# Replacing one of sixteen gathers per block by one-hot products on TensorE, in both layers of a graph network

## The chip, the cores and the metric

The kernel runs on one core of one Trainium2 chip. The metric is the device time of one execution, in microseconds (us), as the median of several. The engines of the core are called PE (TensorE), DVE (VectorE), ACT (ScalarE), POOL (GpSimd, which here issues the indirect DMAs) and SP (SyncE, which here issues nearly all other DMAs).

## The reference

A two-layer graph network with residuals: 6250 nodes of 128 features, 200000 edges `src -> dst`, sorted by `dst`. Everything is float32.

```python
h = jnp.maximum(_layernorm(x, axis=-1), 0.0)
x = x + _L0_gnn_ref(h, src, dst, W, attn_l, attn_r, bias)     # attention, 8 heads of 16
h = jnp.maximum(_layernorm(x, axis=-1), 0.0)
x = x + _L1_gnn_ref(h, edge_attr_4, edge_attr_8, ...)         # tensor product messages

# _L0_gnn_ref
z = (feat @ W).reshape(N, HEADS, PER_HEAD)
el = jnp.einsum('nhp,hp->nh', z, attn_l)
er = jnp.einsum('nhp,hp->nh', z, attn_r)
e = jax.nn.leaky_relu(el[src] + er[dst], negative_slope=NEG_SLOPE)
emax = jax.ops.segment_max(e, dst, num_segments=N)
a = jnp.exp(e - emax[dst])
denom = jax.ops.segment_sum(a, dst, num_segments=N)
agg = jax.ops.segment_sum(z[src] * a[:, :, None], dst, num_segments=N)
out = agg / jnp.maximum(denom, 1e-09)[:, :, None] + bias

# _L1_gnn_ref: s, v = up-projected node features; h = two silu layers on 8 edge features; tpw = h @ A3
mji = concat([ss*y_s*w0, dot(vs, y_v)/R3*w3, ss*y_v*w1, vs*y_s*w2])   # per edge, 256 numbers
message = jax.ops.segment_sum(mji, receiver, num_segments=num_nodes) / 10.0
# then two output projections
```

What matters here is that both layers need, for every edge, the row of a node table at the edge's source: `z[src]` with `el[src]` (136 numbers) in layer 0, `s, v` at `src` (128 numbers) in layer 1. The sources are random.

## The kernel before

**Tiling.** The edges are cut into 1563 tiles of 128 (one edge per partition) and these into 98 blocks of 16 tiles (`KB`). Since edges are sorted by destination, a block's destinations lie in a window of 128 nodes, and two blocks complete one tile of 128 nodes. Segment sums are products with one-hot matrices: `one_hot` (L1097) compares the block's local destination numbers with a row of 0 to 127, and `sums` (L1234, layer 0) or `sums1` (L1570, layer 1) multiplies that with the weighted rows, summing a block in a PSUM bank.

**Rows of the sources.** The node table of layer 0, `t0`, is computed at the start and written to DRAM, 544 bytes a row; that of layer 1, `t1`, is written tile after tile while layer 0 ends its nodes. `gather` (L833) is one indirect DMA on POOL per tile: 128 rows to 128 partitions. `take_rows` issues a block's gathers three steps ahead in layer 0 and two in layer 1, into the five buffers of `z_pool`; block 0 has a buffer of its own, and layer 1's first 24 tiles use another, early table with late corrections. In every third block (`by_row`: 3, 6 up to 93) tile 15 is not gathered: SP fetches its 128 rows by 128 plain DMAs whose addresses come from registers, loaded 32 at a time (`rows_by_row`, L1078). `rows_until` paces this at 42.67 rows per block, so that it is done some eight blocks before the layer's end, and `filled` (ACT) copies the rows to their place.

**Order of the work.** In both loops PE, DVE, ACT and SP execute in the order in which the program writes the instructions; POOL has its own order, of gathers. A step g of layer 0's loop works on four blocks at once:

- block g: `logits` (L1176 to L1179, needs the gathered rows and `er` at the destination), `maxima`;
- block g−1: `neighbours`, `weights`, `weighted` (L1229), `sums`, and, in every second step, the end of a node tile (`node_x` to `node_s`, `node_out` writing `t1` and `t1z`, L1298);
- block g+1: `masks_of`, `turned` (L1151, L1153: the sixteen one-hots of the block are transposed on PE, four to a bank, and cast by ACT), `er_of` (products of the turned one-hots with `er3`);
- block g+2: `ends_of`, the one-hots on DVE.

On SP a step issues: rows, the last node tile's writes, the load of a tile of `x` (L1239, into `x_all`, which stays in SBUF), rows. Layer 1 goes by units of four tiles: `network` for the next block (L1516, L1520), `tensor_weights` (L1533, L1537), `messages` (L1553 to L1562), `sums1` (L1570), and `node1`.

**Before the loops**, tables and masks are prepared: `a1p` (L1001) and the destinations `d_c` (L1025), `d_i` are loaded, local destinations and masks formed (L1141 picks a block's masks by a product).

Of the kernel before, what the change touches and what calls it, by code (L numbers as in the profile page):

```python
# [741 lines left out]
def tile_even_edges(  # L742
# [88 lines left out]
    def gather(to, table, tiles, width, first=0):  # L831
        for k, t in enumerate(tiles, first):
            nc.gpsimd.indirect_dma_start(  # L833
                out=to[:, k, :width], out_offset=None, in_=table,
                in_offset=bass.IndirectOffsetOnAxis(ap=src_col[:, t : t + 1], axis=0))
        return to
# [128 lines left out]
def even_edges(tc, v):  # L965
# [7 lines left out]
    with ExitStack() as ctx:  # L973
        const = ctx.enter_context(tc.tile_pool(name="fconst", bufs=1))
        z_pool = ctx.enter_context(tc.tile_pool(name="fz", bufs=5))
        s_pool = ctx.enter_context(tc.tile_pool(name="fs", bufs=16))
        row_pool = ctx.enter_context(tc.tile_pool(name="frow", bufs=3))
        of_l0 = ctx.enter_context(ExitStack())
        l0c = of_l0.enter_context(tc.tile_pool(name="l0c", bufs=1))

# [14 lines left out]
        x_all = const.tile([P, NX, P], F32, name="fx_all")  # L995
# [8 lines left out]
        a3p = const.tile([P, 2, P], F32, name="fa3p")  # L1004
        nc.sync.dma_start(a3p, v["a3p"])
# [4 lines left out]
        wout = const.tile([P, 2, P], F32, name="fwout")  # L1010
        nc.sync.dma_start(wout, v["wout"])
        dloc = const.tile([P, NB * KB], F32, name="fdloc")
        identb = l0c.tile([P, P], BF, name="fidentb")
        nc.vector.tensor_copy(identb, ident)
# [8 lines left out]
        with tc.tile_pool(name="fbuild", bufs=1) as build:  # L1023
# [10 lines left out]
            nc.vector.tensor_sub(dloc[:, :TU], d_c, off)  # L1034

# [20 lines left out]
        with tc.tile_pool(name="fat_ps", bufs=1, space=PSUM) as at_ps:  # L1056
            col = l0c.tile([P, P], F32, name="fcol")
# [36 lines left out]
        def one_hot(t, m, iota=iota):  # L1094

            s = s_pool.tile([P, 4, P], F32, name="s")
# [20 lines left out]

        in_order = {mybir.EngineType.PE, mybir.EngineType.DVE, mybir.EngineType.Activation,
                    mybir.EngineType.SP}
        with tc.manual_schedule(engines=in_order), \  # L1120
                tc.tile_pool(name="l0", bufs=2) as l0, \
                tc.tile_pool(name="l0n", bufs=2) as l0n, \
                tc.tile_pool(name="l0_ps", bufs=1, space=PSUM) as l0_ps:
# [3 lines left out]
            p_n = l0_ps.tile([P, 512], F32, name="p_n")  # L1127
            er_p, iota_p = p_n[:, P : 2 * P].rearrange("p (t h) -> p t h", h=H), p_n[:, 3 * P :]
            nc.scalar.copy(iota_p, iota)

# [14 lines left out]

            def turned(c, q):
                if 4 * q < c["kt"]:
                    m = min(4, c["kt"] - 4 * q)
                    p_d = l0_ps.tile([P, 4, P], F32, name="p_d", bufs=2)
                    for k in range(m):  # L1150
                        nc.tensor.transpose(p_d[:, k, :], c["s"][q][:, k, :], ident)  # L1151
                    d = c["d", q] = l0.tile([P, 4, P], BF, name="d", bufs=4)
                    nc.scalar.copy(d[:, :m], p_d[:, :m])  # L1153
# [17 lines left out]
            def logits(c, bank="pe"):  # L1171
# [3 lines left out]
                pe = c["pe"] = p_n if bank == "p_n" else l0_ps.tile([P, 512], F32, name=bank, bufs=2)  # L1175
# [61 lines left out]

            def node_rows(i, n):
                nc.sync.dma_start(x_all[:, i : i + n, :],  # L1239
                                  xp[i * P : (i + n) * P].rearrange("(j p) f -> p j f", p=P))  # L1240

            def with_bias(i, n):
                x_i = x_all[:, i : i + n, :]
                nc.vector.tensor_add(x_i, x_i, bias_b[:, None, :].to_broadcast([P, n, F]))

            def node_x(u):
                i, n, agg = u["i"], u["n"], u["agg"]
                x_i = x_all[:, i : i + n, :]
# [14 lines left out]
            def node_h(u):  # L1263
                i, n = u["i"], u["n"]
                rs, mr = normal(l0n, u["mv"], u["rs"], n, f"n{n}")
                xn = u["xn"] = l0n.tile([P, 2, P], F32, name="xn")
                nc.scalar.activation(xn[:, 0, :], x_all[:, i, :], AF.Identity, bias=mr[:, 0, :],
                                     scale=rs[:, 0, :])
                if n == 2:
                    nc.vector.tensor_scalar(xn[:, 1, :], x_all[:, i + 1, :], u["mv"][:, 1, 0:1],  # L1270
                                            rs[:, 1, :], op0=OP.subtract, op1=OP.mult)

            def node_t(u):
                n = u["n"]
                u["p_n"] = p_n.rearrange("p (j f) -> p j f", f=P)
                for j in range(n):
                    nc.tensor.transpose(u["p_n"][:, j, :], u["xn"][:, j, :], ident)
                h_t = u["h_t"] = l0n.tile([P, 2, P], F32, name="h_t")
                nc.scalar.activation(h_t[:, :n], u["p_n"][:, :n], AF.Relu)
# [11 lines left out]
            def node_out(u):  # L1291
                i, n, sv = u["i"], u["n"], u["sv"]
                first = i * P - W0
                for table in (t1, t1z) if i < LATE else (t1,):
                    if i == 0:
                        nc.sync.dma_start(table[: P - W0, :], sv[W0:, 0, :])
                    else:
                        nc.sync.dma_start(  # L1298
                            table[first : first + n * P].rearrange("(j p) f -> p j f", p=P), sv)

# [12 lines left out]
            def take_rows(g):  # L1313
                if 0 < g < NG:
                    c = cs[g]
                    t = c["b"] * KB + c["o"]
                    c["z"] = gathered(t0, range(t, t + c["kt"] - (c["b"] in by_row)), ZW)
# [28 lines left out]
            for g in range(1, 3):  # L1346
                take_rows(g)
            masks_of(cs[0])
# [12 lines left out]
            for i in range(2):  # L1361
                node_rows(i, 1)
            for g in range(NG - 3):
# [3 lines left out]
                for n in late:  # L1367
                    node_out(n)
                if g % 2 == 0 and g // 2 + 2 < NX - 2:
# [6 lines left out]
                logits(c)  # L1376
                ends_of(n2, 0)
# [3 lines left out]
                maxima(c)  # L1381
                ends_of(n2, 1)
# [5 lines left out]
                er_of(n1, 0)  # L1388
                if b4:
                    weights(b4)  # L1390
                for n in nodes:
# [3 lines left out]
                if b4:  # L1395
                    bank_of(b4)
                    weighted(b4, 0)
                turned(n1, 3)
                er_of(n1, 2)
                if b4:  # L1400
                    weighted(b4, 8)
                for n in nodes:
# [4 lines left out]
                if b4:  # L1407
                    sums(b4, 0)
                for n in nodes:
# [7 lines left out]
                if b4:  # L1417
                    sums(b4, 8)
                if g == NG - 4:
# [68 lines left out]
        with tc.manual_schedule(engines=in_order), \  # L1488
                tc.tile_pool(name="l1", bufs=3) as l1, \
                tc.tile_pool(name="l1n", bufs=2) as l1n, \  # L1490
                tc.tile_pool(name="l1_ps", bufs=2, space=PSUM) as l1_ps:

# [8 lines left out]
            def network(b, step):  # L1501
# [7 lines left out]
                if step == 3 or 2 * q0 + 8 >= KT[b] and second:  # L1509
                    c["yp"] = held[:, P + b % 3 * KB * 3 : P + (b % 3 + 1) * KB * 3].rearrange(  # L1510
# [61 lines left out]

            def node1(i, agg):
# [274 lines left out]
```

## Time and profile before

| | |
|---|---|
| time, median of 3 | 3887.06 us (3886.89 to 3891.37) |
| the profiled execution: its own time | 3888.67 us |
| its span, first to last instruction | 3886.9 us |
| mean granted PE clock, share of full | 0.803 |
| gathers and their line | 3024 at L833 in groups of g, 2856.7 us |
| PE, DVE, ACT, POOL busy | 2848.8, 2224.5, 1396.8, 2913.0 us |
| rows by register on SP | 3968 a layer, 0.5 KB each |

How to read it. The busy line gives the time in which each engine executed, its share of the span, and its number of instructions (x). PEld is the loading of weights on PE, beside the matmuls. In the row of slices the span is cut in 40 parts, and a digit is the busy share in tenths; PEclk is the granted clock of PE in tenths. In a row of a group, `L833 POOL DMA_INDIRECT g<-ft,fsrc x3024 | 2856.7, 945 | 922.4 <-issue 858.3` reads: line, engine, operation, output and inputs by the program's names, count, then busy us and mean ns of one, then the idle time of the engine just before these instructions and what ended most of it; "issue" is time in which the engine waited for nothing that the profile shows. Tile numbers are left out of names: `ft` stands for the tables t0 and t1, `r` for the rows by register. A row of waits gives engine, tile, line and who released it, then us in total, times, and the longest. SP's issuing is no busy time on the page; its queue (SPq) is seen in the timeline, whose rows give start and length in us.

### The profile page before, as it was taken

How to read it: one execution, taken by the hardware profiler on the slowest of the kernel's cores; microseconds unless marked ns; L12 is line 12 of the kernel's file. 1: busy time of each engine (PE TensorE's matmuls, PEld its weight loads, DVE VectorE, ACT ScalarE, POOL GpSimd, SP SyncE). 2: the span in 40 equal slices, each digit the busy share in tenths (PEclk: the TensorE clock that was granted, in tenths of full speed). 3: DMA queues.
4: the chain of work that ended last, by engine and by line, in shares of the span. 5: the costliest groups of instructions: out<-in, count | busy, mean ns of one | idle time of the engine just before them, and what ended most of it. 6: DMA issues, size and time to landing. Idle time of an engine off the chain costs nothing. (4 is left out here: it accounts for less than half of the span.)

```text
span 3886.9 us, 62701 instructions
## 1 busy us (share of the span) xinstructions
PE 2848.8 (73%) x14785; PEld 2401.2 (62%) x14785; DVE 2224.5 (57%) x5408; ACT 1396.8 (36%) x3612; POOL 2913.0 (75%) x3096
## 2 busy tenths in 40 slices
PE   3766666666666766666678888888877777778777
PEld 3656656656556656666666666666666556656665
DVE  5544444444444444444457777677766666666666
ACT  3323232323322323232324444444444444444443
POOL 6777777777777777777777777777777777777776
PEclk6666666666666566666689999999999999999999
DMA  6222222222222222222222222222222222222221
GB/s 181 59 64 64 62 64 64 64 62 64 62 64 62 64 61 64 62 64 62 61 61 61 61 62 62 62 62 62 62 62 62 62 62 61 63 60 63 61 61 50
DMA packets 195262, 252.65 MB, mean 65 GB/s; under 512 B 78656, under 2 KB 145088, under 8 KB 194880
## 3 DMA queue, kind: packets, MB, share of 16 engines
q0 software_dynamic: 98048, 207.27, 22.6%
q1 hardware_dynamic: 96544, 41.19, 4.1%
q8 instruction: 120, 1.97, 0.2%
q14 instruction: 262, 2.15, 0.2%
q10 hardware_dynamic: 288, 0.07, 0.0%
HBM read 234.73 MB, written 13.25 MB: 64 GB/s over the span
## 5 line engine op out<-in xcount | busy, mean ns | idle before, releaser
L833 POOL DMA_INDIRECT g<-ft,fsrc x3024 | 2856.7, 945 | 922.4 <-issue 858.3
L1570 PE MATMUL p_u<-mj,s 128*128 128x256 f32 x3126 | 789.9, 397 | 217.9 <-DVE mj L1562 216.5
L1570 PEld LDWEIGHTS p_u<-mj,s 128*128 128x128 f32 x3126 | 588.9, 196 | 385.7 <-DVE mj L1562 310.9
L1234 PE MATMUL p_u<-g,s 128*128 128x136 f32 x3062 | 597.8, 376 | 0.4 <-DVE g L1229 0.4
L1234 PEld LDWEIGHTS p_u<-g,s 128*128 128x128 f32 x3062 | 572.1, 279 | 0.5 <-DVE g L1229 0.4
L1537 ACT ACTIVATE p_w<-p_w,yb 128x64 f32<-128x64 f32 x1563 | 450.3, 288 | 121.5 <-PE p_w L1533 80.4
L1553 DVE TENSOR_TENSOR vy<-g,p_i 128x384 f32<-128x384 f32 x387 | 212.9, 550 | 366.6 <-DMA g<-ft,fsrc 258.0
L1533 PE MATMUL p_w<-fa3p,h 128*128 128x256 f32 x1564 | 412.0, 387 | 0.0
L1151 PE MATMUL p_d<-fident,s 128*128 128x128 f32 x1563 | 384.7, 411 | 0.0
L1533 PEld LDWEIGHTS p_w<-fa3p,h 128*128 128x128 f32 x1564 | 289.4, 195 | 118.1 <-issue 52.5
L1176 DVE TENSOR_TENSOR e_s<-g,p_n 128x128 f32<-128x128 f32 x96 | 27.5, 286 | 578.6 <-DMA g<-ft,fsrc 566.2
L1518 ACT ACTIVATE h<-p_h,fb 128x512 f32<-128x512 f32 x196 | 134.6, 687 | 573.2 <-PE p_h L1516 571.8
L1151 PEld LDWEIGHTS p_d<-fident,s 128*128 128x128 f32 x1563 | 312.4, 225 | 37.6 <-issue 26.3
L1144 ACT COPY mk<-p_m 128x385 f32<-128x385 f32 (+1 forms) x99 | 47.6, 481 | 781.3 <-PE p_m L1141 781.2
L1229 DVE TENSOR_TENSOR g<-g,pe 128x1024 f32<-128x1024 f32 x193 | 225.5, 1209 | 129.2 <-ACT g L1220 126.4
L1153 ACT CAST d<-p_d 128x512 bf16<-128x512 f32 x391 | 228.8, 586 | 192.0 <-PE p_d L1151 141.6
L1179 PE MATMUL pe<-fident,e_s 128*128 128x128 f32 x98 | 39.1, 399 | 326.2 <-DVE e_s L1177 326.2
L1097 DVE TENSOR_TENSOR s<-p_n,fdloc 128x512 f32<-128x512 f32 x391 | 266.1, 682 | 6.7 <-ACT sv L1289 3.4
L1097 DVE TENSOR_TENSOR s<-p_i,fdloc 128x512 f32<-128x512 f32 x391 | 266.1, 681 | 3.8 <-ACT p_i L1512 3.8
L1516 PE MATMUL p_h<-ft,fa1p 128*128 128x128 f32 x1568 | 217.2, 283 | 63.3 <-DMA ft<-in_e_f_dram 63.1
L1516 PEld LDWEIGHTS p_h<-ft,fa1p 128*128 128x128 f32 x1568 | 210.6, 198 | 83.9 <-issue 65.3
L1523 ACT ACTIVATE h<-p_h,fb 128x512 f32<-128x512 f32 x196 | 134.7, 687 | 307.1 <-PE p_h L1520 307.1
(202 smaller groups left out, 3344.3 us busy)
## 6 DMA issues: line engine op xcount, KB each, us to landing
r<-ft SPq DMA_DIRECT2D x3968, 0.5 KB
r<-ft SPq DMA_DIRECT2D x3968, 0.5 KB
g<-ft,fsrc POOLq DMA_INDIRECT x3024
ft<-in_e_f_dram SPq DMA_DIRECT2D x98, 64.0 KB
yb<-in_e_y_dram SPq DMA_DIRECT2D x98, 32.0 KB
fx_all<-in_e_xp_dram SPq DMA_DIRECT2D x48, 64.0 KB
out_dram<-fx_all SPq DMA_DIRECT2D x47, 64.0 KB
ft<-sv SPq DMA_DIRECT2D x46, 64.0 KB
```

The source lines that it names most:

```text
L833: nc.gpsimd.indirect_dma_start(out=to[:, k, :width], out_offset=None, in_=table, in_offset=bass.IndirectOffsetOnAxis(ap=src_col[:, t : t + ...
L1097: nc.vector.tensor_tensor(s[:, :m], iota[:, None, :].to_broadcast([P, m, P]), dloc[:, t : t + m].unsqueeze(2).to_broadcast([P, m, P]), OP. ...
L1151: nc.tensor.transpose(p_d[:, k, :], c["s"][q][:, k, :], ident)
L1153: nc.scalar.copy(d[:, :m], p_d[:, :m])
L1229: nc.vector.tensor_mul(zh, zh, p_a[:, k0 : k0 + m].unsqueeze(3).to_broadcast([P, m, H, D]))
L1234: nc.tensor.matmul(c["p_u"][:, :ZW], c["s"][k // 4][:, k % 4, :], c["z"][:, k, :], start=c["o"] + k == 0, stop=c["o"] + k == KT[c["b"]] - 1)
L1516: nc.tensor.matmul(p_h[:, q, :], a1p[:, q0 + q, :], c["ft"], start=True, stop=True)
L1523: nc.scalar.activation(h2, p_h, AF.Silu, bias=b2)
L1533: nc.tensor.matmul(w[:, k : k + n].rearrange("p k a u -> p (k a u)"), c["h2"][q // 4][:, q % 4, :], a3p[:, :n].rearrange("p k f -> p (k f) ...
L1537: nc.scalar.activation(w[:, k, ::2, :], w[:, k, ::2, :], AF.Copy, scale=c["yb"][:, k0 + k, 0:1])
L1553: nc.vector.tensor_mul(vy, v_n, y_p)
L1570: nc.tensor.matmul(blk[b]["p_u"][:, :MW], u["s"][:, k, :], u["mj"][:, k, :], start=k0 + k == 0, stop=k0 + k == KT[b] - 1)
```

## The change

**Products in place of a gather.** In 44 blocks of layer 0 (`dense`: from block 27 on, those not in `by_row`) and in 20 of layer 1 (`dense1`: 16, 20, up to 92), tile 14 (`KD`) is no longer gathered. Its 128 rows are made by products. `spread` lays the tile's source numbers along the free axis by a product; `ends_to` compares them with the node numbers of 17 ranges and gives 17 one-hot matrices in bf16; `rows_of` multiplies each with the table, which lies in SBUF in three bf16 parts whose sum is the float32 number: 17 x 3 matmuls, each with up to three node tiles as columns (48 with 408 columns and 3 with 272 in layer 0; 384 and 256 in layer 1), summed in bank `p_x`. `taken` picks the right one of the three node tiles by three masks on DVE and writes the rows in place. In layer 0 this is spread over two steps, in layer 1 over five units (`dense_step`).

**The tables in three parts.** `node_tiles` loads two node tiles on SP, `in_three` splits them by two copies on ACT and two subtractions on DVE: a pair per step in the first 25 steps of layer 0, a pair per two units in the first 50 units of layer 1, with the load issued a step or four units ahead.

**The turned ends.** In layer 0 `turned` no longer transposes and casts. Four comparisons on DVE (128x512) compare a broadcast of the block's destinations with the partition's number. The broadcast is a load on SP per block, `ends_row`: a row of 4096 bytes of a new DRAM table `fends_d` to all 128 partitions, two buffers, issued after `logits` two blocks ahead. The table is written at the start, from a subtraction on DVE.

**Other moves.** `x` is no longer held in SBUF for both layers: layer 0 loads a tile per node tile and writes the sum to a DRAM table `fx1`, from which layer 1 loads it. Constant rows and columns that products need are held in a PSUM bank of their own. Some pools and constants move to the layer that uses them.

```diff
     def gather(to, table, tiles, width, first=0):
-        for k, t in enumerate(tiles, first):
+        for t in tiles:
+            k = first + t - tiles[0]
...
+            d_b = build.tile([P, TG, P], BF, name="fd_b")
...
+            nc.vector.tensor_sub(d_b, d_i, off_t.unsqueeze(2).to_broadcast([P, TG, P]))
+            nc.sync.dma_start(ends.rearrange("g t e -> t g e"), d_b)
...
+        NR = -(-NX // 3)
+        KD = KB - 2
+        order = sorted(range(NR), key=lambda k: (k > 0, 2 * NR + k < NX, k))
+        half = (NR + 1) // 2
+        dense = {b for b in range(NX // 2 + 2, NB - 4) if b not in by_row}
+        dense1 = set(range(NX // 4 + 4, NB - 4, 4))
...
+        def node_tiles(pool, table, width, i, n, bufs=2):
+            zr = pool.tile([P, 2, width], F32, name="zr", bufs=bufs)[:, :n]
...
+                nc.sync.dma_start(zr, rest.rearrange("(j p) f -> p j f", p=P))
+            return zr
+
+        def in_three(pool, zr, width, t_s, i, n):
+            r = pool.tile([P, 2, width], F32, name="zr2", bufs=1)[:, :n]
+            nc.scalar.copy(t_s[:, 0, i : i + n, :], zr)
+            nc.vector.tensor_sub(r, zr, t_s[:, 0, i : i + n, :])
+            nc.scalar.copy(t_s[:, 1, i : i + n, :], r)
+            nc.vector.tensor_sub(t_s[:, 2, i : i + n, :], r, t_s[:, 1, i : i + n, :])
...
+            def spread(c):
+                b = c["b"]
+                nc.tensor.matmul(at_p, key[:, b : b + 1].to_broadcast([P, P]), ident,
+                                 start=True, stop=True)
...
+            def ends_to(c, h):
+                n = half if h == 0 else NR - half
+                oh = c["oh", h] = ohs[:, h * half : (h + 1) * half, :]
+                nc.vector.tensor_tensor(
+                    oh[:, :n], at_p.unsqueeze(1).to_broadcast([P, n, P]),
+                    place[:, h * half : h * half + n].unsqueeze(2).to_broadcast([P, n, P]), OP.is_equal)
...
+                for k in range(k0, min(k0 + n, NR)):
+                    i = order[k]
+                    m = len(range(i, NX, NR))
+                    for s in range(3):
+                        nc.tensor.matmul(c["p_x"][:, :m, :], c["oh", k // half][:, k % half, :],
+                                         t0s[:, s, i::NR, :], start=k == 0 and s == 0,
+                                         stop=k == NR - 1 and s == 2)
...
+            def taken(c):
+                b, z = c["b"], c["z"][:, KD, :]
+                nc.vector.tensor_scalar(z, c["p_x"][:, 0, :], part[:, b, 0:1], None, op0=OP.mult)
+                for r in (1, 2):
+                    nc.vector.scalar_tensor_tensor(z, c["p_x"][:, r, :], part[:, b, r : r + 1], z,
+                                                   op0=OP.mult, op1=OP.add)
...
+            def ends_row(b):
+                if b < NB:
+                    to = ends_row.tiles[b] = l0.tile([P, KB, P], BF, name="er_d", bufs=2)
+                    g, j = divmod(b, P // KB)
+                    nc.sync.dma_start(to, ends[g : g + 1, j * KB : (j + 1) * KB, :].to_broadcast([P, KB, P]))
...
             def turned(c, q):
...
-                    p_d = l0_ps.tile([P, 4, P], F32, name="p_d", bufs=2)
-                    for k in range(m):
-                        nc.tensor.transpose(p_d[:, k, :], c["s"][q][:, k, :], ident)
-                    d = c["d", q] = l0.tile([P, 4, P], BF, name="d", bufs=4)
-                    nc.scalar.copy(d[:, :m], p_d[:, :m])
+                    d = c["d", q] = l0.tile([P, 4, P], BF, name="d")
+                    k0 = c["o"] + 4 * q
+                    nc.vector.tensor_tensor(d[:, :m], ends_row.tiles[c["b"]][:, k0 : k0 + m],
+                                            node_p.unsqueeze(2).to_broadcast([P, m, P]), OP.is_equal)
...
-                    c["z"] = gathered(t0, range(t, t + c["kt"] - (c["b"] in by_row)), ZW)
+                    c["z"] = gathered(t0, [k for k in range(t, t + c["kt"])
+                                           if not (c["b"] in by_row and k % KB == KB - 1)
+                                           and not (c["b"] in dense and k % KB == KD)], ZW)
...
+            for b in range(2):
+                ends_row(b)
...
+            asked(0)
             for g in range(NG - 3):
                 take_rows(g + 3)
                 filled(0, g, cs[g]["z"], ZW)
                 rows_until(rows, g + 0.5)
                 for n in late:
                     node_out(n)
+                asked(g + 1)
                 if g % 2 == 0 and g // 2 + 2 < NX - 2:
                     node_rows(g // 2 + 2, 1)
                 rows_until(rows, g + 1)
...
                 logits(c)
+                ends_row(g + 2)
+                to, was = n2["b"] in dense, n1["b"] in dense
+                if to:
+                    spread(n2)
                 ends_of(n2, 0)
...
                 maxima(c)
+                if to:
+                    ends_to(n2, 0)
+                if was:
+                    rows_of(n1, half, 4)
...
+                if was:
+                    rows_of(n1, half + 4, NR)
                 if b4:
                     weights(b4)
+                if was:
+                    taken(n1)
...
+                split(g)
...
+            def dense_step(b, q):
+                if b + 1 in dense1:
+                    if q == 1:
+                        dense_ends(b + 1)
+                    elif q > 1:
+                        dense_rows(b + 1, (q - 2) * 4, 4)
+                if b in dense1:
+                    dense_rows(b, 8 + 3 * q, 3)
+                    if q == 2:
+                        dense_taken(b)
...
                 messages(u)
+                dense_step(b, k0 // 4)
                 late_rows(4 * (i + 1))
```

## The prediction

> **What bounds the kernel now.** I read first the page's busy line and slices, for the engine without a pause, and its costliest groups.
>
> ```profile
> span 3886.9 us, 62701 instructions
> PE 2848.8 (73%) x14785; PEld 2401.2 (62%) x14785; DVE 2224.5 (57%) x5408; ACT 1396.8 (36%) x3612; POOL 2913.0 (75%) x3096
> POOL 6777777777777777777777777777777777777776
> PEclk6666666666666566666689999999999999999999
> L833 POOL DMA_INDIRECT g<-ft,fsrc x3024 | 2856.7, 945 | 922.4 <-issue 858.3
> L1229 DVE TENSOR_TENSOR g<-g,pe 128x1024 f32<-128x1024 f32 x193 | 225.5, 1209 | 129.2 <-ACT g L1220 126.4
> L1151 PE MATMUL p_d<-fident,s 128*128 128x128 f32 x1563 | 384.7, 411 | 0.0
> L1153 ACT CAST d<-p_d 128x512 bf16<-128x512 f32 x391 | 228.8, 586 | 192.0 <-PE p_d L1151 141.6
> L1097 DVE TENSOR_TENSOR s<-p_n,fdloc 128x512 f32<-128x512 f32 x391 | 266.1, 682 | 6.7 <-ACT sv L1289 3.4
> ```
>
> POOL has the same 7 in every slice: its gathers take 0.945 us and 0.30 between two. The waits say whether those 0.30 are a wait, and the timeline of POOL how evenly they go.
>
> ```profile
> POOL g L833 <- issue: 860.1, 2820, 0.3
> DVE e_s L1176 <- DMA g<-ft,fsrc: 568.2, 91, 9.2
> 164.07 0.94 POOL L833 DMA_INDIRECT g<-ft,fsrc  x1 [0.31 <-issue]
> ```
>
> POOL waits for nobody, never over 0.3 us; the computation waits for gathers (e_s, 91 of 96 steps). One gather costs 1.249 us (starts 162.82 and 164.07), and they run from 42.6 to 3866.9; 20 us of tail follow. So time = start + gathers x 1.249 + stalls of POOL + 20. A block of 16 tiles takes POOL 20.0 us, one of 15 18.7; before, a third of layer 0's have 15, 19.6 on average.
>
> Next, what lies underneath: busy time by windows (window, length, PE, PEld, DVE, ACT, POOL, clock, DMA share, GB/s), one of each layer.
>
> ```profile
> 1200.00:1500.00 300.00, 199.45 (x1173) 183.09 (x1173) 136.15 (x296) 89.19 (x203) 226.77 (x241) 0.65 0.28 63
> 2900.00:3200.00 300.00, 237.90 (x1100) 183.14 (x1099) 202.25 (x515) 124.55 (x351) 226.81 (x241) 0.99 0.24 62
> ```
>
> Last SP's queue, by the timeline: two stretches of layer 0 and two of the start. It issues by register one row after another for every third block (L1078).
>
> ```profile
> 48.67 0.43 SPq L1001 DMA_DIRECT2D fa1p<-in_e_a1p_dram  x1
> 54.22 0.33 SPq L1025 DMA_DIRECT2D fd_c<-in_e_dstc_dram  x1
> 70.93 59.43 SPq L1078 DMA_DIRECT2D r<-ft  x152
> ...
> 1199.77 0.42 SPq L1239 DMA_DIRECT2D fx_all<-in_e_xp_dram  x1
> 1202.51 33.51 SPq L1078 DMA_DIRECT2D r<-ft  x88
> 1237.62 0.38 SPq L1298 DMA_DIRECT2D ft<-sv  x1
> ```
>
> And one line of SP's waits:
>
> ```profile
> SPq L1025 <- DMA fa1p<-in_e_a1p_dram: 0.7, 1, 0.7
> ```
>
> From one ft write to the next is a pair of blocks, 39 us, of which rows take 34: SP is nearly as full as POOL, though the page gives it no share. 26 rows from 1203.90 took 8.31 us: 0.3235 a row, and 2.3 us of register load stand between 1200.19 and 1202.51.
>
> **What the skill says.** "TensorE: Matmul & The Clock Gate", Back-to-back issue gap: an isolated matmul of N columns takes N/1.2 ns cold and N/2.4 + 2.5 warm; Part 1 of that page: the clock is half until the array has been busy for some 3.4 us. The trace agrees that there are two clocks: 0.65 in layer 0, 0.99 in layer 1. "DMA: Bandwidth & Descriptors", Anatomy of one DMA: about 2.0 us fixed plus bytes at 436 GB/s, given for the gathers' path; this trace has no broadcast load to compare.
>
> **The change, part by part.**
>
> Gathers: 44 blocks of layer 0 and 20 of layer 1 lose tile 14's: 64 x 1.249 = −79.9 us. Layer 0's dense blocks (27 on) and its by-row ones then all take 18.7.
>
> Products, layer 0: 48 matmuls of 408 columns and 3 of 272: 48 x 172.5 + 3 x 115.8 = 8.6 us warm, 17.0 cold, an estimate from the skill's gap. The 16 transposes leave (1563 x 0.246 us of summed occupancy = 384.7, 3.9 a block). PE's 199.45/300 x 19.6 = 13.0 us a block falls to 9.1 and averages, with two of three dense, 14.8 to 20.5 of the 18.7. I take the low end: the longer matmul work holds the clock up. DVE: 136.15/300 x 19.6 = 8.9, plus four comparisons for the turned ends at 0.68 (L1097) 2.7, plus two thirds of (2.55 for one-hots, by L1229's 1.18 ns an element scaled, and 3 x 0.29 for taking) 2.3: 13.9 of 18.7. ACT loses four casts. All of this is hidden under the gathers, at 18.7 a block; without that cover dense steps would cost the excess each. Layer 1: PE 15.5 + 8.4/4 = 17.6, DVE 13.2 + 0.9, of 19.3: hidden, and nothing is charged. Splitting tables (two copies, two subtractions a pair, some 2 us on two engines) lies there too.
>
> Start: the ends row of block 2 (er_d, 512 KB written on SBUF) is issued in step 0 behind 172 rows, where nothing that the computation needed stood behind rows. Rows start later, since the table of ends is written first, its two broadcasts, two x and two zr loads follow: 84.5 instead of 70.93, an estimate. 152 rows take 59.4 (the row above): 144; zr and x 0.9; 20 rows and a register load 8.7: 153.6; er_d(2). Then 44 rows, a register load and a zr, 17.9: er_d(3) at 171.5, landed 175. Step 2's comparisons wait for it, and behind them on DVE that step's maxima and weights of block 1; 12 us later, block 1's sums end, about 187. Before, they ended at 127.84 (the timeline of PE: 122.38 plus 5.46), with 36 us to spare until POOL needed that buffer for block 6, at 164.4. Now POOL stands for 187 − 164 = **+23 us** (bounds 10 to 35: less if rows start by 72, more if the broadcasts share the rings with gathers badly).
>
> SP in layer 0, per pair of blocks: 85.33 rows x 0.3235 + 2.67 register loads x 2.29 = 33.7. Before, three plain DMAs of 0.47: 35.1 of 39.1. After, two er_d and an x1 write more: 36.5, and with two zr of the split (first 25 steps) 37.4; POOL's pair falls to 37.5 from block 27. That leaves one microsecond for stalls, and there is one: in the built program each load on SP waits for the load eight places ahead of it. The wait above is this one: fd_c is the eighth load after fa1p. Behind er_d stand seven loads, 7 x 0.3235 + 0.47 = 2.7 us of issue; a broadcast that takes L to land stalls SP by about 2/3 (L − 2.7) + 1/3 max(0, L − 5.0), the third being where a register load falls between. L from both sides: 3.2 (skill: 2.0 + 512 KB/436 GB/s, an estimate) and 5.5 (fa1p, also 512 KB, on a crowded start: from 48.67 to 54.2). I take 3.9: 0.8 a stall, 36.5 + 1.6 − 37.5 = 0.63 over, times 32 dense pairs until the rows are done: **+20 us**. The split stretch gives 37.4 + 1.6 = 39.0 of 39.1: nothing.
>
> Turn to layer 1: with SP as pace the computation lags POOL by up to 40 us, of which it catches up all but some 11 once rows end at block 89; layer 1's first gather needed t1 with 4 us to spare (1983.38 the last write, 1989.35): **+7** (0 to 15), +1 for reloading weights. Layer 1's SP: 18.3 + 0.94 of 19.6, no charge.
>
> Sum on the profiled execution, 3888.7: −79.9 + 23 + 20 + 8 = −29, 3859.8; it lies 1.6 above the median, 3887.1, so **3858**.
>
> **The rivals.**
> Gathers alone set it (SP hides, L under 3.5): start and turn remain, 3887 − 80 + 10 to 31 = 3817 to 3838. For it: SP's gap of 3.6 us a pair now, the skill's 3.2. Against: one microsecond is little.
> SP becomes the bound and the kernel slower: mechanism, the landing of er_d on SP's ring of eight, in every step of layer 0. At L = 4.4 the loss is 41 + 7 + 31 = 79, nothing won; from 4.6 slower by over 0.2%; at 5.0 it is 83 + 31 − 80, 3921; at 5.5, 3965. For it: fa1p's 5.5. Against: that one shared the rings with some twenty loads.
> Dense steps bound by PE at the cold clock, or by the chain in a step: at 20.0 us a step 67 x 1.27 = 85 more, about 3920. For it: 0.65 in layer 0, and products stand in PE's order ahead of the sums. Against: 14.8 warm. It decides at 18.7.
> The change doesn't do what it says: gathers are counted by the trace, 3000 instead of 3064; no way to see it fail.
>
> **How the numbers follow.** SP paces layer 0 mildly (L 3.5 to 4.3): 50%, 3840 to 3878. Gathers alone: 20%. SP heavy: 20%, 3880 to 3960. PE or chain: 10%. The likeliest gives 3858. The range 3812 to 3925 leaves out about one in fourteen below and one in eight above. ±0.2% (3879.3 to 3894.9) is what a measurement here tells from no change. Faster: 20% and most of the first 50, with a few of the last 10: 0.66. Same: 0.10, from around L = 4.4. Slower: 0.24, the rest of SP and PE.
>
> **What would show it.** Right: L833 has 3000-odd gathers and a stall of about 23 us ahead of block 6's first, near 165 to 190; short ones by blocks 30 to 89 whose releaser is the computation, behind DVE comparisons that wait for DMA er_d; SP's row stretches stand end to end. Layer 1's windows hold 1.249 a gather with DVE and PE below 19.3 a block. Wrong: POOL never idle (SP hides); or the comparisons never wait for er_d while sums or PE set the step; or the second half of layer 0 at a clock of 0.65 with PE busy all over; or layer 1 with stalls, where I charge none.

## The result, and where the time went

| | before | after |
|---|---|---|
| time, median of 4 | 3887.32 us (3886.89 to 3891.37) | 4022.84 us (4019.5 to 4023.69) |
| span of the profiled execution | 3886.9 us | 4021.7 us |
| gathers on POOL | 3064 | 3000 |
| stalls of POOL between gathers (starts further apart than 1.249 us) | 2.7 us | 218.2 us |

The changed kernel is slower: ratio 1.0343, 95% interval 1.0327 to 1.036. The forecast was 3858, faster. Some of the kernels below fell on chips on which the kernel before itself took 6220 to 6333 us, and no time of theirs is used.

The page of the kernel after: span, busy line, slices of POOL and of the clock, then groups by cost.

```profile
span 4021.7 us, 67085 instructions
PE 2921.8 (73%) x16614; PEld 2289.9 (57%) x16614; DVE 2710.7 (67%) x6269; ACT 1223.9 (30%) x3322; POOL 2856.3 (71%) x3032
POOL 6577776777777777777775546777777777777776
PEclk6566667888888888888787889999999999999999
L834 POOL DMA_INDIRECT g<-ft,fsrc x2960 | 2799.7, 946 | 1109.9 <-issue 932.5
L1272 DVE TENSOR_TENSOR d<-er_d,p_i 128x512 bf16<-128x512 bf16 x391 | 264.2, 676 | 291.2 <-DMA er_d<-fends_d 289.6
L1232 PE MATMUL p_x<-t0s,fz_first 128*128 128x408 bf16 (+1 forms) x2244 | 459.9, 357 | 0.0
```

POOL's even row of sevens has two dents: one digit near the start, and four slices, `5546`, from about 2110 to 2510 us. That is early in layer 1. Layer 0 shows only a 6, from about 600 to 700 us, where the first blocks with products begin. From there on the clock in layer 0 is mostly 8 of 10.

The waits of the kernel after (engine, tile, line, releaser: us in total, times, longest):

```profile
POOL g L834 <- issue: 934.7, 2775, 12.1
POOL g L834 <- DVE mj L1720: 81.5, 13, 12.8
POOL g L834 <- PE p_m L1253: 29.9, 1, 29.9
DVE zr L1169 <- ACT t1s L1168: 152.7, 23, 8.7
SPq L1082 <- DMA er_d<-fends_d: 77.2, 60, 2.1
SPq L1162 <- DVE zr L1169: 82.8, 15, 8.9
```

The waits of its gathers of g were 0.3 us at most before; now there are one of 29.9 and a dozen of about 12. The starts of the gathers, taken one after another along POOL's timeline, give the stalls by stretch, each against 1.249 us a gather:

- 29.6 at one place near the start, and 1.0 more than before ahead of it;
- 56 in layer 0 after that (8 before block 27's stage, 48 after);
- 10 at the turn to layer 1;
- 118 between layer 1's 60th and 290th gather, and nothing in the rest.

Stalls grew by 218.2 - 2.7 = 215.5. Less the gathers saved, 64 x 1.249 = 79.9, less 1.0 since the first one starts earlier, and with a tail 0.2 longer, that is 134.8, and the spans differ by 134.8.

**The start** is as forecast in kind. SP's queue, DVE and POOL by the timeline:

```profile
87.80 58.63 SPq L1082 DMA_DIRECT2D r<-ft  x152
...
156.30 0.36 SPq L1263 DMA_DIRECT2D er_d<-fends_d  x1
...
160.23 0.69 DVE L1272 TENSOR_TENSOR d<-er_d,p_i 128x512 bf16<-128x512 bf16 x1 [56.38 <-DMA er_d<-fends_d]
...
193.69 0.94 POOL L834 DMA_INDIRECT g<-ft,fsrc  x1 [29.93 <-PE p_m L1253]
```

The ends row of block 2 stands behind 172 rows and is issued at 156.3; DVE has stood for 56 us for it and goes on 3.9 us later, and POOL gets block 6's buffer at 193.7.

**Layer 0** shows the sign that the prediction named for SP's pace: DVE's comparisons wait for the ends row, once for the 56.4 us of the start and 66 times more.

```profile
DVE d L1272 <- DMA er_d<-fends_d: 289.6, 67, 56.4
```

**Layer 1** is where the forecast charged nothing. Two units of the stretch, by the timelines of DVE, ACT and PE:

```profile
2216.10 0.43 DVE L1169 TENSOR_TENSOR zr<-zr,t1s 128x256 f32<-128x256 f32 x1 [6.82 <-ACT t1s L1168]
2217.00 0.42 DVE L1171 TENSOR_TENSOR t1s<-zr,t1s 128x256 bf16<-128x256 f32 x1 [0.47 <-ACT t1s L1170]
2217.53 0.55 DVE L1711 TENSOR_TENSOR vy<-g,p_i 128x384 f32<-128x384 f32 x1
...
2214.50 1.25 ACT L1695 ACTIVATE p_w<-p_w,yb 128x64 f32<-128x64 f32 x4 [0.18 <-PE p_w L1691]
2215.68 0.40 ACT L1168 CAST t1s<-zr 128x256 bf16<-128x256 f32 x1
...
2210.82 1.89 PE L1728 MATMUL p_u<-mj,s 128*128 128x256 f32 x8
2212.54 1.05 PE L1674 MATMUL p_h<-ft,fa1p 128*128 128x128 f32 x8
2213.43 1.03 PE L1691 MATMUL p_w<-fa3p,h 128*128 128x256 f32 x4
2220.16 3.78 PE L1728 MATMUL p_u<-mj,s 128*128 128x256 f32 x8 [5.70 <-DVE mj L1720]
```

Read backwards: DVE's messages (2217.53) stand behind the split's first subtraction (2216.10), which has waited 6.82 us for ACT's copy (2215.68). That copy stands in ACT's order behind the scaling of the next unit's weights (2214.50), which needs PE's products of weights (2213.43), and these stand in PE's order behind the sums of the unit before (2210.82), which needed DVE's messages of that unit. So in every second unit DVE, PE and ACT run one after another, where before they overlapped. PE also runs slower after such a wait: its eight sums took 3.78 us at 2220.16, and 1.89 at 2210.82. The windows say the same (columns as in the prediction; the kernel before, then after, in the same stretch):

```profile
2147.00:2451.00 304.00, 256.25 (x1164) 203.20 (x1163) 215.52 (x552) 131.61 (x372) 229.90 (x244) 0.95 0.24 62
```

```profile
2147.00:2451.00 304.00, 191.54 (x722) 147.16 (x721) 147.38 (x376) 97.42 (x272) 147.64 (x157) 0.81 0.18 48
2451.00:3800.00 1349.00, 1247.97 (x6195) 973.47 (x6195) 1031.56 (x2561) 601.09 (x1681) 1019.60 (x1081) 0.99 0.25 64
```

In 304 us POOL issued 157 gathers instead of 244, while no engine was busy for even two thirds of the time: the sign of a chain of waits, not of an engine that is full. From 2451 on, when the last table tile has been split, the layer has its products and still 1081 gathers in 1349 us, 1.248 each.

### The profile page after: what moved, and what is told of

The parts are those of the page before. It is cut to its first block, busy times and chain, and to the rows that moved or that the text cites. A ratio compares the mean times of both kernels' runs of the same rounds, so it can differ in the third digit from the quotient of the medians.

```text
span 4021.7 us, 67085 instructions
## 1 busy us (share of the span) xinstructions
PE 2921.8 (73%) x16614; PEld 2289.9 (57%) x16614; DVE 2710.7 (67%) x6269; ACT 1223.9 (30%) x3322; POOL 2856.3 (71%) x3032
## 5 line engine op out<-in xcount | busy, mean ns | idle before, releaser
L834 POOL DMA_INDIRECT g<-ft,fsrc x2960 | 2799.7, 946 | 1109.9 <-issue 932.5
L1101 DVE TENSOR_TENSOR s<-p_i,fdloc 128x512 f32<-128x512 f32 x782 | 533.5, 683 | 145.0 <-PE p_i L1208 133.4
L1354 PE MATMUL p_u<-g,s 128*128 128x136 f32 x3062 | 509.5, 335 | 0.3 <-DVE g L1349 0.3
L1354 PEld LDWEIGHTS p_u<-g,s 128*128 128x128 f32 x3062 | 484.3, 240 | 2.1 <-DVE g L1349 0.4
L1272 DVE TENSOR_TENSOR d<-er_d,p_i 128x512 bf16<-128x512 bf16 x391 | 264.2, 676 | 291.2 <-DMA er_d<-fends_d 289.6
L1232 PE MATMUL p_x<-t0s,fz_first 128*128 128x408 bf16 (+1 forms) x2244 | 459.9, 357 | 0.0
L1232 PEld LDWEIGHTS <-fz_first 128*128 128x128 bf16 x2244 | 225.6, 103 | 153.5 <-issue 25.3
L1282 PEld LDWEIGHTS <-d 128*128 128x128 bf16 x1563 | 95.6, 116 | 263.6 <-DVE d L1272 259.5
L1715 DVE TENSOR_REDUCE vd<-vy 128x128 f32<-128x384 f32 x391 | 228.9, 586 | 0.0
L1716 DVE TENSOR_TENSOR mj<-p_w,yb 128x384 f32<-128x384 f32 x391 | 213.8, 547 | 0.0
```

Source lines behind the costliest of these rows:

```text
L834: nc.gpsimd.indirect_dma_start(out=to[:, k, :width], out_offset=None, in_=table, in_offset=bass.IndirectOffsetOnAxis(ap=src_col[:, t : t + ...
L1101: nc.vector.tensor_tensor(s[:, :m], iota[:, None, :].to_broadcast([P, m, P]), dloc[:, t : t + m].unsqueeze(2).to_broadcast([P, m, P]), OP. ...
L1232: nc.tensor.matmul(c["p_x"][:, :m, :], c["oh", k // half][:, k % half, :], t0s[:, s, i::NR, :], start=k == 0 and s == 0, stop=k == NR - 1 ...
L1272: nc.vector.tensor_tensor(d[:, :m], ends_row.tiles[c["b"]][:, k0 : k0 + m], node_p.unsqueeze(2).to_broadcast([P, m, P]), OP.is_equal)
L1354: nc.tensor.matmul(c["p_u"][:, :ZW], c["s"][k // 4][:, k % 4, :], c["z"][:, k, :], start=c["o"] + k == 0, stop=c["o"] + k == KT[c["b"]] - 1)
L1715: nc.vector.tensor_reduce(vd, vy.rearrange("p t i u -> p t u i"), AX.X, OP.add)
```

## The experiments

All start from the changed kernel. Two questions: whether layer 1's 118 us come from the wait for ACT or from the split's loads and work; and whether layer 0's 56 us come from SP's queue or from the products on PE and DVE. The runs m1 to m4 shared runs of the kernel before at 3890.08 us (3887.79 to 3890.51), k1 one of 3894.31. k1, m1, m2 and m3 were executed once each, m4 four times.

**k1: the split after the messages.**

```diff
-                if i % 2 == 0:
-                    if zrs: in_three(...)
-                    if i + 4 < NX: zrs.append(node_tiles(...))
                 messages(u)
+                if i % 2 == 0:
+                    if zrs: in_three(...)
+                    if i + 4 < NX: zrs.append(node_tiles(...))
```

> Layer 1's split and its load stand after the unit's messages instead of ahead of them; engines and amounts are the same. Theory (DVE waits for a copy that stands in ACT's order behind the scaling of the next unit's weights, so the units run one after another; the place in DVE's order makes that wait costly): POOL's 118 us of stalls between layer 1's 60th and 290th gather fall below 25, 3905 to 3930. Rivals (the amount of work, or the loads of table tiles on SP and what they hold up): the stalls stay, 4000 or more.

Measured: 3942.83 us, layer 1's stalls 37 instead of 118. The waits:

```profile
DVE zr L1169 <- ACT t1s L1168: 82.6, 23, 10.1
POOL g L834 <- DVE mj L1720: 26.6, 11, 5.7
```

The place is most of it, since work and loads are unchanged. But the stalls are not below 25 and the time is not within 3905 to 3930, as the theory had said. DVE still waits for ACT, now with the next unit's one-hots and messages behind it; the theory had taken the wait for harmless once the messages were ahead of it.

**m1: the copies on DVE.** No engine waits for another within the split; place, loads and amounts stay, and DVE gets two copies of 128x256 more.

```diff
-        def in_three(pool, zr, width, t_s, i, n):
+        def in_three(pool, zr, width, t_s, i, n, copy=nc.scalar.copy):
-            nc.scalar.copy(t_s[:, 0, i : i + n, :], zr)
+            copy(t_s[:, 0, i : i + n, :], zr)
...
-                        in_three(l1d, zrs.pop(0), P, t1s, i, min(2, NX - i))
+                        in_three(l1d, zrs.pop(0), P, t1s, i, min(2, NX - i), nc.vector.tensor_copy)
```

> Layer 1's split of the table keeps its place and its loads, but its two copies are made by DVE instead of ACT. Theory (the cost is DVE's wait for ACT, and moving the split after the messages took away only the larger part of it): POOL's 118 us of stalls between layer 1's 60th and 290th gather fall below 10, the time to about 3907. Rival (the loads of table tiles on SP, or the amount of work): the stalls stay at the 37 us that the moved split left, or higher: 3940 to 4025.

Measured: 3905.69 us, stalls in the stretch 2.9. The window of the stretch, and the wait that remains at the start:

```profile
2147.00:2451.00 304.00, 260.71 (x1221) 201.72 (x1219) 244.26 (x621) 130.87 (x368) 230.26 (x242) 0.97 0.27 70
POOL g L834 <- PE p_m L1253: 30.8, 1, 30.8
```

DVE does more, 244 us instead of 147, and POOL has its 242 gathers. The theory holds to 2 us of time: without DVE's wait for a copy in ACT's order, 115 of the 118 us are gone. SP's wait for table buffers (82.8 us in the changed kernel) is gone without touching a load, so it was a consequence.

**m3: layer 0 without the products' work.** `spread`, `ends_to` and `rows_of` do nothing, and

```diff
             def taken(c):
-                b, z = c["b"], c["z"][:, KD, :]
-                nc.vector.tensor_scalar(z, c["p_x"][:, 0, :], part[:, b, 0:1], None, op0=OP.mult)
...
+                nc.vector.memset(c["z"][:, KD, :], 0.0)
```

> Layer 0 without the products' work: no spread, one-hots or matmuls; the 44 tiles are not gathered either but set to zero by one DVE operation, so their messages are left out of the result. Splitting, ends rows and SP's queue are as in the changed kernel. Theory (SP paces layer 0): its stalls of 48 us in the stretch with dense blocks stay, to within 10: 4012 to 4025. Rival (the products' chain sets the step): they go, about 3975.

Measured: 4013.83 us, within the theory's range; layer 0's stalls after the start are 10 + 42 instead of 8 + 48. The windows of layer 0's stretch with dense blocks, after and m3:

```profile
650.00:1860.00 1210.00, 860.86 (x5978) 642.29 (x5977) 841.89 (x1669) 230.49 (x582) 879.57 (x931) 0.84 0.35 90
```

```profile
650.00:1860.00 1210.00, 546.69 (x3783) 510.40 (x3783) 701.60 (x1508) 231.15 (x585) 883.28 (x936) 0.67 0.35 90
```

PE falls from 860.86 busy us to 546.69, DVE by 140, and POOL gains 5 gathers in 1210 us. DVE waits for the ends row all the more, 91 times instead of 67 (L1245 here is L1272 of the changed kernel):

```profile
DVE d L1245 <- DMA er_d<-fends_d: 584.6, 91, 56.8
```

So the products do not set layer 0's step: without them DVE stands for a load that SP issues late. The products also pay for part of themselves: the clock is 0.84 with them and 0.67 without.

**m2: the ends row issued by ACT.**

```diff
-                    nc.sync.dma_start(to, ends[g : g + 1, ...].to_broadcast([P, KB, P]))
+                    nc.scalar.dma_start(to, ends[g : g + 1, ...].to_broadcast([P, KB, P]))
```

> The broadcast of a block's destinations is issued by ACT instead of SP, at the same place in the step. Theory (SP paces layer 0): the stall of 29.6 us at the start goes, since the load no longer stands behind rows, and of layer 0's 56 us of short stalls at least 40 go, since SP's pair falls by 0.9 of issue and by its waits for the landing: 3935 to 3955. Rival (the products' chain on PE and DVE sets layer 0's step): only the start goes, 3990 to 4000. Layer 1's 118 us stay under both.

Measured: 4232.55 us, 210 slower than the changed kernel. Neither theory had this sign. At the start the stall fell from 29.6 to 10.4, since the load no longer stands behind rows. It did not go: the split's first load of a table tile in the loop (zr, issued at 156.48) stands behind 152 rows on SP as well, and DVE's subtraction waited 43.4 us for ACT's copy of it. Layer 0's stalls grew from 56 to 284. The waits of m2, on SP and DVE:

```profile
SPq L1082 <- DMA er_d<-fends_d: 379.2, 83, 11.8
DVE d L1272 <- DMA er_d<-fends_d: 2.7, 1, 2.7
DVE zr L1169 <- ACT t0s L1168: 190.1, 24, 43.4
```

the waits of ACT and DVE for the rows by register, from 200 to 2000 us:

```profile
ACT g L1096 <- DMA r<-ft: 214.8, 19, 16.5
DVE e_s L1296 <- ACT g L1096: 285.3, 18, 23.3
```

and two rows of ACT's timeline:

```profile
1007.55 0.33 ACTq L1263 DMA_DIRECT2D er_d<-fends_d  x1
1015.06 0.48 ACT L1256 COPY mk<-p_m 128x385 f32<-128x385 f32 x1 [10.55 <-PE p_m L1253]
```

The rows on SP wait for the broadcast on ACT's queue, 379 us in all instead of 77, though they need nothing of it: the wait for the load eight places back counts the loads of both queues in the program's order. (For one broadcast issued at 1078.15, SP stood from its row at 1070.94 to 1081.76.) ACT reaches its issue only when its own work allows, and part of that work, the copy L1096 of rows by register, waits for SP's rows. So the two queues wait for each other, and the rows come late to DVE. SP waits 302 us more, and POOL stands 227 more in layer 0, less 19 at the start.

**m4: both edits** of m1 and m2.

> Both repairs: layer 1's copies of the split on DVE, and the ends row issued by ACT. Theory: of 218 us of stalls some 30 are left, 3830 to 3845, below the kernel before by 1.2%. If the products' chain sets layer 0's step: 3875 to 3885.

Measured: 4116.31 us, 1.0585 of the kernel before (1.0567 to 1.0603), far from the 3830 to 3845 expected: it is m2 less 116, as m1 is the changed kernel less 117. The effects of the two edits add, and the repair of SP is none.

**Runs that tell nothing.** The same edits as m1, k1 and m2 had first been run as e1, e2, e4, those of k1, m2 and m3 as f1, f3 and f4, and k1's again as g1, on the chips named above: 6210 to 6573 us where the kernel before took 6220 to 6321. Five other edits ran on such chips only. The changed kernel itself did not run there, so nothing is concluded from these times, and the expectations of the five stay open.

e1, the edit of m1: 6372.1 against 6233.13.

> Layer 1's split of the table keeps its place and its loads, but its two copies are made by DVE instead of ACT. Theory (DVE waits for a copy that stands in ACT's order behind the scaling of the next unit's weights, which stands behind PE's sums of the unit before, so the units run one after another): POOL's 118 us of stalls between layer 1's 60th and 290th gather fall below 10, the time to about 3907. Rival 1 (the loads of table tiles on SP and their buffers hold edge loads and rows up): nothing changes, 4010 to 4025. Rival 2 (other edits of layer 1: the node product in the held bank, one-hots in five buffers): nothing changes either.

e2, f1 and g1, the edit of k1: 6399.9 against 6233.13, 6392.03 against 6220.2, 6505.91 against 6321.32.

> Layer 1's split and its load stand after the unit's messages instead of ahead of them; engines and amounts are the same. Theory (the place in DVE's order makes the wait costly): the stalls fall from 118 to under 25 us, 3905 to 3930. If it is the amount of work or the loads, they stay: 4000 or more.

> Layer 1's split and its load stand after the unit's messages instead of ahead of them; engines and amounts are the same. Theory (DVE waits for a copy that stands in ACT's order behind the scaling of the next unit's weights, so the units run one after another; the place in DVE's order makes that wait costly): POOL's 118 us of stalls between layer 1's 60th and 290th gather fall below 25, 3905 to 3930. Rivals (the amount of work, or the loads of table tiles on SP and what they hold up): the stalls stay, 4000 or more.

> Layer 1's split and its load stand after the unit's messages instead of ahead of them; engines and amounts are the same. Theory (DVE waits for a copy that stands in ACT's order behind the scaling of the next unit's weights, so the units run one after another; the place in DVE's order makes that wait costly): POOL's 118 us of stalls between layer 1's 60th and 290th gather fall below 25, 3905 to 3930. Rivals (the amount of work, or the loads of table tiles on SP and what they hold up): the stalls stay, 4000 or more. On a chip where the kernel before is itself far from 3887 neither number holds, and only the wait's own row is read.

e4 and f3, the edit of m2: 6571.63 against 6233.13, 6573.03 against 6220.2.

> The broadcast of a block's destinations is issued by ACT instead of SP, at the same place in the step. Theory (SP paces layer 0): the stall of 29.6 us at the start goes, since the load no longer stands behind rows, and of layer 0's 56 us of short stalls at least 40 go, since SP's pair falls by 0.9 of issue and by its waits for the landing: 3935 to 3955. Rival (the products' chain on PE and DVE sets layer 0's step): only the start goes, 3990 to 4000. Layer 1's 118 us stay under both.

> The broadcast of a block's destinations is issued by ACT instead of SP, at the same place in the step. Theory (SP paces layer 0): the stall of 29.6 us at the start goes, since the load no longer stands behind rows, and of layer 0's 56 us of short stalls at least 40 go, since SP's pair falls by 0.9 of issue and by its waits for the landing: 3935 to 3955. Rival (the products' chain on PE and DVE sets layer 0's step): only the start goes, 3990 to 4000. Layer 1's 118 us stay under both.

f4, the edit of m3: 6210.01 against 6220.2.

> Layer 0 without the products' work: no spread, one-hots or matmuls; the 44 tiles are not gathered either but set to zero by one DVE operation, so their messages are left out of the result. Splitting, ends rows and SP's queue are as in the changed kernel. Theory (SP paces layer 0): its stalls of 48 us in the stretch with dense blocks stay, to within 10: 4012 to 4025. Rival (the products' chain sets the step): they go, about 3975.

No products in layer 1, e3 and f2: `dense1 = set()`, no split and no loads of it. 6299.66 against 6233.13, 6296.17 against 6220.2.

> Layer 1 without products: no split, no loads of table tiles, all 20 gathers back; the other moves of layer 1 (node product in the held bank, x loaded from DRAM, five buffers of one-hots) stay. Theory: the 118 us go, 20 gathers of 1.249 come back, 4023 - 118 + 25 = 3930. Rival 2 (those other moves are the cause): the stalls stay, about 4048.

> Layer 1 without products: no split, no loads of table tiles, all 20 gathers back; the other moves of layer 1 (node product in the held bank, x loaded from DRAM, five buffers of one-hots) stay. Theory: the 118 us go, 20 gathers of 1.249 come back, 4023 - 118 + 25 = 3930. Rival (those other moves are the cause): the stalls stay, about 4048.

k1's and m2's edits together (h1): 6662.81 against 6333.38.

> Two edits together: layer 1's split after the unit's messages, and the broadcast of destinations issued by ACT instead of SP. Theory: 4023 less 95 to 118 of layer 1's stalls, less 30 at the start, less 40 to 50 of layer 0's stalls: 3830 to 3860, below the kernel before. Rival (the products' work sets the step in layer 0): 3880 to 3905. Rival (layer 1's stalls come from the amount of work or from SP's loads): 3935 to 3960.

A shorter lead of the rows (n1), `(block + 1)` for `(block + 3)` in `rows_until` for layer 0, with m1's edit: 6431.12 against 6315.18.

> Layer 1's split on DVE, as in m1, and in layer 0 the rows by register start with a lead of one block instead of three: 64 and 21 rows ahead of the ends row of block 2 instead of 152 and 20. Theory: the stall ahead of block 6's first gather, 30 us, falls below 3; the rows last two blocks longer, at most 4 us more of layer 0's stalls: 3905.7 - 28 = 3876 to 3882. If something else than the place behind rows holds the start up: 3900 or more.

A small ends row (n2), `to[:, :1, :]` loaded and read sixteen times, with m1's edit: 6482.26 against 6315.18.

> Layer 1's split on DVE, as in m1, and the ends row's load brings one tile of sixteen (32 KB to SBUF instead of 512), which all sixteen comparisons read, so that layer 0's attention uses wrong ends. SP's number of issues stays. Theory (SP's waits for the landing of these loads, 77 us in the changed kernel, carry layer 0's pace over POOL's): layer 0's 54 us of stalls fall below 15, the start's 30 stay: 3860 to 3872. Rival (the issue of rows and loads alone fills SP): they fall by less than 15, 3890 or more.

Rows for every fourth block (n3), `b % 4 == 3` in layer 0 and products for the other three, with m1's edit and a lead of two: 6425.13 against 6315.18.

> Layer 1's split on DVE; in layer 0 rows by register for every fourth block only and products for the other three of four from block 27 on, with a lead of two blocks: SP's pair of blocks falls by 7 us, two gathers more in all. Theory (SP alone paces layer 0): start and stalls go, 3905.7 - 30 - 50 + 3 = 3829, to 3840. Rival (with SP relieved, the products' chain, now in three of four blocks, sets the step): 3860 to 3880.

So no version was found that is faster than the kernel before: m1, the best, stands 15.6 us above it in its one execution. That the start's 30 us and layer 0's 56 can be had back is not shown.

## Why the prediction was wrong

**The model held.** Time is the start, gathers x 1.249, stalls and a tail: the stalls and gathers give the difference of the two spans. (The prediction let the gathers of the kernel before end at 3866.9; the last one starts at 3870.95, so the tail is 15 us rather than 20, in both kernels.) The 79.9 us for 64 gathers were there. Of some 164 us between the forecast and the measured change, 118 lie in layer 1, 36 in SP's pace, 7 at the start and 2 at the turn.

**The step that failed** is "Splitting tables (two copies, two subtractions a pair, some 2 us on two engines) lies there too", with "Layer 1's SP: 18.3 + 0.94 of 19.6, no charge": 118 us. It costed the split by its busy time on each engine and set that against a mean share of busy time. What it left out is the rule that the prediction applied to er_d: for a wait, name what is queued behind it and what the releaser itself is queued behind. The subtraction waits for ACT, ACT's copy stood behind the next unit's weights, and DVE's messages stood behind the subtraction. In layer 0 the same helper stands at the end of a step, and DVE waited 25.1 us for it in all, beside SP's pace. m1 shows that this wait is all but 3 us of it. The prediction did name the sign: "layer 1 with stalls, where I charge none". Without this loss the kernel would still not be faster: m1, which hardly has it, takes 3905.69 us, so the next term counts for the sign too.

**SP's pace in layer 0**: right mechanism, term too small, 56 instead of 20. SP's instructions of the 1100 us from 700 on, added up one by one, are rows, register loads, plain DMAs and waits for er_d, and hardly 6 us of waits for computation. So SP is full. Sixty ends rows were issued between 690.7 and 1854.3, so a pair of blocks takes 38.8 us instead of the 38.1 worked out.

The waits for er_d were sized well. In those 1100 us 2418 rows take 851.8 us with these waits; at 0.3325 us a row without them, 48 us are left over 57 loads, 0.84 each, where 0.8 was taken. The one landing that was read off, at the start, took 3.9 us, as taken. The row by register was not sized well: 0.3235 us came from 26 undisturbed rows, while the mean in the kernel before, over 1000 us from 700 on, is 733.4 us for 2206, 0.3325. 85 rows x 0.009 is 0.8 a pair, on a margin that was one microsecond. Over 32 dense pairs that is 25 us, and 8 more over the ten pairs before, which were to cost nothing. What is left, some 3 us, is not traced.

m3 supports the mechanism from one side: without products SP issues 2421 rows in those 1100 us, with them 2418, and DVE waits the longer for the ends row. m2 supports it from the other: with SP's rows later, POOL stands longer. No run relieved SP, so how much of the 56 us that would give back is open.

**The start**: 29.6 for 23. Rows began at 87.8 instead of 84.5, the load stood at 156.3 instead of 153.6, block 1's sums ended at 192.9 instead of 187. The place behind the rows as cause rests on the trace and on m2, where 19 of the 29.6 us went with er_d's place and a load of the split was left behind the rows. The prediction had listed the split's load there and charged only its issue.

**The turn** cost 10 for 8. **Products** were hidden but for a little: without those of layer 0 the kernel is 9 us faster, and they took 459.9/44 = 10.5 us of PE a block, between the ends of 8.6 and 17.0 and nearer to the low one.

**The rivals.** SP as the bound of a slower kernel was the rival on that side, with its price at L = 4.4 and above; L was 3.9, and the larger part of the loss, layer 1's 118 us, stood in no rival. The dense steps bound by PE at the cold clock did not come: 0.84. (The 0.65 and 0.99 that the prediction read as two clocks are means over 300 us. In windows of 5 us the kernel before shows the two themselves: 0.50 from 1205 to 1210 us, 1.00 from 1235 to 1240.)

## What to carry to other kernels

Work that is small on every engine can still cost the sum of all engines' steps, if it puts a wait for one in-order engine in front of another's main work: walk the cycle of orders (who stands behind the waiting instruction, and behind what does its releaser stand) before calling it hidden. If a helper hops between engines, put all of it on the one that has the slack. Walk the same cycle before moving a load to another engine's queue: if that engine waits for the first queue, the two can come to wait for each other, as in m2. And where a queue is within a few per cent of the pace, take the price of its commonest instruction from the mean over a long stretch and not from a clean one.

## What the runs showed of the hardware that was not expected

Moving a load from SP's queue to ACT's did not take its landing out of SP's way: SP's waits for it rose from 77.2 us (60 times) to 379.2 (83 times), since in the built program each load waits for the one eight places back over both queues; a wait for it on the queue that it left was not expected. And matmuls of 408 bf16 columns between others, with PE busy for 860.86 us of 1210 instead of 546.69, raised the granted clock of the stretch from 0.67 (m3) to 0.84, and other matmuls got shorter: `sums` in layer 0 take 335 ns on average in the changed kernel, 366 in m3 and 376 before.
